# A two-layer graph network on one core: layer 1 with att applied to x1 before W, and the first layer's attention with queries on partitions

## The chip, the cores and the metric

The kernel runs on one core of a Trainium2 chip. A core has a matrix engine (TensorE, PE in the profile; its weight loads are listed apart as PEld), VectorE (DVE), ScalarE (ACT), GpSimd (POOL), a queue engine for transfers (SyncE, SP) and 16 DMA engines. [...]

The metric is the device time of one execution in microseconds, the median of several runs.

## The reference

64 batch elements of 256 tokens with 512 features, everything in float32, one 256x256 adjacency matrix for all of them. Layer 0 is masked attention with 8 heads of 64, layer 1 a graph attention with one score per token. Cut to what matters:

```python
# layer 0
q, k, v = x @ Wq + bq, x @ Wk + bk, x @ Wv + bv      # in 8 heads of 64
scores = q k^T / 8 + (1 - adj) * -1e9
out = softmax(scores) v
x1 = layernorm(x + out @ Wo + bo)

# layer 1
h = x1 @ W
s1, s2 = h @ a[:512], h @ a[512:]
e = leaky_relu(s1[:, None] + s2[None, :], 0.2) * adj
att = softmax(e)
y = layernorm(x1 + elu(att @ h + beta * h))
```

Since h = x1 W, `att @ h + beta * h` equals `((att + beta I) @ x1) @ W`, and `h @ a` equals `x1 @ (W a)`.

## The kernel before

The kernel is written with a framework that takes tiles from named pools (`bufs` is the number of buffers of a tag), finds the dependences itself and sets the semaphores. The program is unrolled completely. The order in which the steps are written gives instructions their priority; the order in which they stand on an engine in the profile is not always the written one.

One batch element goes through three parts, each a list of steps:

- `front(b)` (L141): two `tr` steps transpose the two 128-token tiles of x into xT (L126, L127) and add bo to x on GpSimd (L153); eight `qk` steps make one 128-feature block of qT or kT each (L158, evacuated by VectorE with the bias, L159); two `val` steps make v with tokens on partitions (L164, evacuated by ScalarE, L165).
- `attention(b)` (L175): for each of four head pairs a `scores` step computes k q^T, so that keys lie on partitions (L184), takes exp on ScalarE (L187) without subtracting a maximum, multiplies by the transposed 0/1 mask on GpSimd (L188) and adds the two key tiles (L190). A `mix` step multiplies by v (L200), gets the sums over keys from a product with ones (L203), and scales by their reciprocal (L204, L205); the result is written over qT. Probabilities are never transposed here. `check` (L207) keeps the largest and the least reciprocal; after the last element one branch (L373) repeats everything with `attention_general` (L218), which subtracts the row maximum, if a sum was out of range. In the profiled run the branch is not taken.
- `back(b)` (L273): two `proj` steps (product with Wo, L279; add, L280; layer norm, L131 to L138), two `flip` steps that transpose x1 into x1T, two `hidden` steps for h (L291) with the two scores of each token (L297), `edges` (L300 to L319), `flip_att` (L325), and two `last` steps: att h (L332), beta h added (L334), elu (L337 to L340), layer norm, store.

A layer norm takes the statistics and the final scaling on VectorE and, between them, the inverse root on GpSimd (L136, L137).

The loop (L352) has B + 2 = 66 passes. Pass i holds front(i), attention(i-1) and back(i-2); `merged` (L28) interleaves their steps by relative place in their own list. 62 passes hold all three parts. q, k and v biases: bq and bk are added as said; bv is folded into bo once at the start, through Wo (L115, L116).

The PSUM banks: ps_mm 3 (all products with weights), ps_sc 2 (one buffer of two banks), ps_tr 2 (transposes), ps_pv 1 (mix). The weights are loaded once through ScalarE's queue, x and the output move through SP's.

Of the kernel before, what the change touches and what calls it, by code (L numbers as in the profile page):

```python
# [8 lines left out]
F32 = mybir.dt.float32  # L9
# [5 lines left out]
P = 128  # L15
# [4 lines left out]
LARGE = 1e25  # L20
# [14 lines left out]
def gnn_two_layers(ctx: ExitStack, tc: tile.TileContext, x, adj, Wq, bq, Wk, bk, Wv, bv, Wo, bo, W, a, beta, out):  # L35
# [11 lines left out]
    ps_sc = ctx.enter_context(tc.tile_pool(name="ps_sc", bufs=1, space=PSUM))  # L47
# [11 lines left out]
    def load(b, at=None):  # L59
        X[b] = []  # L60
        for t in range(NT):
            xt = xp.tile([P, D], F32, tag="x", name=f"x_{b}_{t}")
            nc.sync.dma_start(xt, (x[b] if at is None else at)[t * P:(t + 1) * P, :])
            X[b].append(xt)
# [24 lines left out]
    bv_sb = by_partition(bv, "bv_sb")  # L89
# [7 lines left out]
    beta_sb = on_all(beta, 0, 1, "beta_sb")  # L97

# [5 lines left out]
    maskT = const.tile([P, NT, N], F32, name="maskT")  # L104
    tr = ps_tr.tile([P, NT, N], F32, tag="tr", name="tr_m")
    for k in range(NT):
        for t in range(NT):
            nc.tensor.transpose(tr[:, k, t * P:(t + 1) * P], mask_sb[:, t, k * P:(k + 1) * P], ident)
    nc.scalar.activation(maskT, tr, AF.Exp)
    ones = const.tile([P, HD], F32, name="ones")  # L110
    nc.gpsimd.memset(ones, 1.0)

    ps = ps_mm.tile([P, D], F32, tag="mm", name="ps_bo")
    for c in range(C):
        nc.tensor.matmul(ps, bv_sb[:, c:c + 1].to_broadcast([P, P]), wo_sb[:, c, :], start=c == 0, stop=c == C - 1)  # L115
    nc.vector.tensor_add(bo_sb, bo_sb, ps)  # L116

    seen = const.tile([P, 2, B], F32, name="seen")
# [22 lines left out]
    def front(b):  # L141
# [13 lines left out]
        def qk(w, bias, dst, m):  # L155
# [3 lines left out]
            nc.vector.tensor_scalar(dst[b][:, m, :], ps, bias[:, m:m + 1], None, ALU.add)  # L159

        def val(t):
# [3 lines left out]
            nc.scalar.copy(V[b][:, t, :], ps)  # L165

        steps = [lambda t=t: tr(t) for t in range(NT)]
        for m in range(C):
            steps.append(lambda m=m: qk(wq_sb, bq_sb, QT, m))
            steps.append(lambda m=m: qk(wk_sb, bk_sb, KT, m))  # L170
# [4 lines left out]
    def attention(b):  # L175
        E, S, rcp = {}, {}, {}

        def scores(hp):

            ps = ps_sc.tile([P, 2, NT, N], F32, tag="sc", name="ps_sc")  # L180
            for k in range(NT):
                for s in range(2):
                    r = s * HD
                    nc.tensor.matmul(ps[:, s, k, :], KT[b][r:r + HD, hp, k * P:(k + 1) * P],  # L184
                                     QT[b][r:r + HD, hp, :], start=True, stop=True)
            E[hp] = work.tile([P, 2, NT, N], F32, tag="E", name=f"E_{b}_{hp}", bufs=3)
            nc.scalar.activation(E[hp], ps, AF.Exp, scale=1.0 / HD ** 0.5)  # L187
            nc.gpsimd.tensor_tensor(E[hp], E[hp], maskT.unsqueeze(1).to_broadcast([P, 2, NT, N]), ALU.mult)  # L188
            S[hp] = work.tile([P, 2, N], F32, tag="S", name=f"S_{b}_{hp}", bufs=3)
            nc.gpsimd.tensor_tensor(S[hp], E[hp][:, :, 0, :], E[hp][:, :, 1, :], ALU.add)  # L190

        def mix(hp):

            if hp == 0:
                rcp[0] = work.tile([P, H // 2, N], F32, tag="rcp", name=f"rcp_{b}")
            ps = ps_pv.tile([P, 2, N], F32, tag="pv", name="ps_pv")
            for k in range(NT):
                for s in range(2):
                    h = 2 * hp + s
                    nc.tensor.matmul(ps[s * HD:(s + 1) * HD, 0, :], V[b][:, k, h * HD:(h + 1) * HD],  # L200
                                     E[hp][:, s, k, :], start=k == 0, stop=k == NT - 1)
# [207 lines left out]
```

## Time and profile before

| what | value |
|---|---|
| median of 3 runs (lowest, highest) | 3621.76 us (3616.07, 3630.26) |
| profiled run, its own time | 3621.76 us |
| its span, first to last instruction | 3620.0 us |
| mean granted TensorE clock | 0.993 |
| ScalarE busy | 886.6 us (24%) |
| HBM traffic | 39.85 MB read, 33.55 MB written, 20 GB/s |

The chain of work that ended last is spread over the engines: TensorE 39%, GpSimd 24%, gaps at issue 22%, VectorE 13%. It follows releases backward from the last instruction and changes engines many times in each of the 66 passes, so for a loop like this one it is better to take one pass apart. The costliest groups on TensorE are the q and k products (503.6 and 497.3 us, 2048 records each, two for every fp32 matmul), and the products with W, Wo and Wv (468.4, 460.6 and 460.3 us, 1024 records each). Record durations overlap: a record of the 256-column form lasts 389 ns but follows its neighbour by about 216 ns.

Views of the profile used below: the page of totals, busy times in chosen stretches, instructions in order of time, who waited for whom, and groups of instructions by line.

### The profile page before, as it was taken

The page shows a single profiled execution, that of the slowest core. Times are in us where ns is not written, and L with a number is a line of the kernel's source. Part 1 is how long each engine was busy: PE and PEld are TensorE (multiplying, and loading weights), DVE is VectorE, ACT ScalarE, POOL GpSimd, SP SyncE. Part 2 cuts the span into 40 slices and gives each one's busy share as a digit, 9 for nine tenths or more (in the row PEclk, how much of TensorE's full clock was granted, in tenths as well). Part 3 has the DMA queues.
Part 4 walks back from the last instruction along what each step waited for, and adds up shares of the span by engine and source line. Part 5 has one row for each costly group of instructions (what it writes and reads, how often), then busy time and mean ns, then how long its engine had stood idle before and what let it go on. Part 6 is the DMA issues. An engine that isn't in the chain of part 4 may idle for free.

```text
span 3620.0 us, 36170 instructions
## 1 busy us (share of the span) xinstructions
PE 3413.8 (94%) x14222; PEld 1961.9 (54%) x14222; DVE 2081.6 (58%) x3335; ACT 886.6 (24%) x1474; POOL 1409.4 (39%) x1231
## 2 busy tenths in 40 slices
PE   7999999999999999999999999999999999999996
PEld 4555555555555555555555555555555555555552
DVE  2565555565655555656555555555565555565655
ACT  1222222222222222222222222222222222222222
POOL 2443433434334334343343343433443433434332
PEclk9999999999999999999999999999999999999998
DMA  2000000000000000000000000000000000000000
GB/s 99 12 24 12 24 24 12 24 21 15 24 12 24 24 12 24 21 15 24 15 21 24 12 24 24 12 24 18 18 24 12 24 24 12 24 20 16 18 9 16
DMA packets 40319, 75.80 MB, mean 21 GB/s; under 512 B 4368, under 2 KB 4624, under 8 KB 40144
## 3 DMA queue, kind: packets, MB, share of 16 engines
q1 hardware_dynamic: 37136, 67.39, 5.5%
q10 hardware_dynamic: 2640, 5.24, 0.4%
q8 instruction: 115, 1.88, 0.2%
q0 software_dynamic: 368, 0.79, 0.1%
q14 instruction: 60, 0.49, 0.0%
HBM read 39.85 MB, written 33.55 MB: 20 GB/s over the span
## 4 chain that ended last, share of the span: by engine, by line
PE 39%; POOL 24%; issue 22%; DVE 13%; ACT 2%; POOLq 0%; ACTq 0%
POOL E L188 12%; PE ps_v L164 12%; PE ps_g L332 7%; PE ps_o L279 6%; POOL S L190 5%; DVE x L138 5%; PE ps_qk L158 3%; PE ps_sc L184 3%; DVE rcp L204 3%; PE tr_x L126 3%; POOL x L153 2%; POOL e L309 2%; POOL rs L137 2%; PE ps_pv L200 2%; ACT E L187 2%
## 5 line engine op out<-in xcount | busy, mean ns | idle before, releaser
L188 POOL TENSOR_TENSOR E<-E,maskT 128x1024 f32<-128x1024 f32 x256 | 600.7, 2347 | 834.9 <-ACT E L187 834.9
L138 DVE TENSOR_SCALAR x<-x,mv,rs 128x512 f32<-128x512 f32 x256 | 325.9, 1273 | 447.0 <-POOL rs L137 447.0
L204 DVE RECIPROCAL rcp<-ps_pv 128x256 f32<-128x256 f32 x256 | 448.2, 1751 | 152.7 <-PE ps_pv L203 152.7
L158 PE MATMUL ps_qk<-xT,wk_sb 128*128 128x256 f32 x2048 | 503.6, 389 | 0.0
L158 PE MATMUL ps_qk<-xT,wq_sb 128*128 128x256 f32 x2048 | 497.3, 386 | 0.2 <-ACT xT L127 0.2
L297 DVE SCALAR_TENSOR_TENSOR junk<-h,a_sb 128x512 f32<-128x512 f32 x256 | 192.6, 788 | 508.6 <-ACT h L293 508.6
L291 PE MATMUL ps_h<-w_sb,x1T 128*128 128x512 f32 x1024 | 468.4, 600 | 0.7 <-ACT x1T L127 0.7
L279 PE MATMUL ps_o<-wo_sb,qT 128*128 128x512 f32 x1024 | 460.6, 593 | 0.0
L164 PE MATMUL ps_v<-wv_sb,xT 128*128 128x512 f32 x1024 | 460.3, 592 | 0.0
L158 PEld LDWEIGHTS ps_qk<-xT,wk_sb 128*128 128x128 f32 x2048 | 373.4, 190 | 139.2 <-issue 99.0
L136 POOL TENSOR_SCALAR rs<-mv 128x1 f32<-128x1 f32 x256 | 56.2, 220 | 929.0 <-DVE mv L134 929.0
L187 ACT ACTIVATE E<-ps_sc 128x1024 f32<-128x1024 f32 x256 | 262.0, 1023 | 631.8 <-PE ps_sc L184 631.8
L158 PEld LDWEIGHTS ps_qk<-xT,wq_sb 128*128 128x128 f32 x2048 | 369.0, 190 | 85.5 <-DVE kT L159 23.8
L190 POOL TENSOR_TENSOR S<-E 128x512 f32<-128x512 f32 x256 | 349.5, 1365 | 15.2
L153 POOL TENSOR_TENSOR x<-x,bo_sb 128x512 f32<-128x512 f32 x128 | 184.1, 1440 | 392.2 <-PE tr_x L126 366.1
L184 PE MATMUL ps_sc<-qT,kT 64*128 64x256 f32 x2048 | 333.1, 405 | 0.1
L164 PEld LDWEIGHTS ps_v<-wv_sb,xT 128*128 128x128 f32 x1024 | 194.5, 190 | 244.0 <-issue 229.0
L291 PEld LDWEIGHTS ps_h<-w_sb,x1T 128*128 128x128 f32 x1024 | 189.5, 190 | 209.3 <-issue 204.9
L184 PEld LDWEIGHTS ps_sc<-qT,kT 64*128 64x128 f32 x2048 | 193.6, 186 | 198.2 <-issue 186.0
L200 PE MATMUL ps_pv<-E,v 128*64 128x256 f32 x2048 | 283.2, 397 | 4.5 <-DVE qT L205 3.2
L279 PEld LDWEIGHTS ps_o<-wo_sb,qT 128*128 128x128 f32 x1024 | 184.9, 190 | 185.9 <-issue 185.4
L332 PE MATMUL ps_g<-h,attT 128*128 128x512 f32 x512 | 254.7, 621 | 1.3 <-ACT attT L327 1.3
(68 smaller groups left out, 2987.2 us busy)
## 6 DMA issues: line engine op xcount, KB each, us to landing
x<-in_x_dram SPq DMA_DIRECT2D x128, 256.0 KB, 2.6
out_dram<-x SPq DMA_DIRECT2D x128, 256.0 KB, 2.0
wq_sb<-in_L_gnn_Wq_dram ACTq DMA_DIRECT2D x1, 1024.0 KB, 6.6
wk_sb<-in_L_gnn_Wk_dram ACTq DMA_DIRECT2D x1, 1024.0 KB, 14.1
wv_sb<-in_L_gnn_Wv_dram ACTq DMA_DIRECT2D x1, 1024.0 KB, 12.1
wo_sb<-in_L_gnn_Wo_dram ACTq DMA_DIRECT2D x1, 1024.0 KB, 8.8
w_sb<-in_L_gnn_W_dram ACTq DMA_DIRECT2D x1, 1024.0 KB, 9.8
a_sb<-in_L_gnn_a_dram POOLq DMA_DIRECT2D x2, 256.0 KB, 8.0
```

The source lines that it names most:

```text
L138: nc.vector.tensor_scalar(xt, xt, mv[:, 0:1], rs, ALU.subtract, ALU.mult)
L158: nc.tensor.matmul(ps, w[:, c, m * P:(m + 1) * P], XT[b][:, c, :], start=c == 0, stop=c == C - 1)
L164: nc.tensor.matmul(ps, XT[b][:, c, t * P:(t + 1) * P], wv_sb[:, c, :], start=c == 0, stop=c == C - 1)
L184: nc.tensor.matmul(ps[:, s, k, :], KT[b][r:r + HD, hp, k * P:(k + 1) * P], QT[b][r:r + HD, hp, :], start=True, stop=True)
L187: nc.scalar.activation(E[hp], ps, AF.Exp, scale=1.0 / HD ** 0.5)
L188: nc.gpsimd.tensor_tensor(E[hp], E[hp], maskT.unsqueeze(1).to_broadcast([P, 2, NT, N]), ALU.mult)
L190: nc.gpsimd.tensor_tensor(S[hp], E[hp][:, :, 0, :], E[hp][:, :, 1, :], ALU.add)
L200: nc.tensor.matmul(ps[s * HD:(s + 1) * HD, 0, :], V[b][:, k, h * HD:(h + 1) * HD], E[hp][:, s, k, :], start=k == 0, stop=k == NT - 1)
L204: nc.vector.reciprocal(rcp[0][:, hp, :], ps[:, 1, :])
L279: nc.tensor.matmul(ps, QT[b][:, c, t * P:(t + 1) * P], wo_sb[:, c, :], start=c == 0, stop=c == C - 1)
L291: nc.tensor.matmul(ps, x1T[0][:, c, t * P:(t + 1) * P], w_sb[:, c, :], start=c == 0, stop=c == C - 1)
L332: nc.tensor.matmul(ps, att[1][:, j, t * P:(t + 1) * P], hs[j], start=j == 0, stop=j == NT - 1)
```

## The change

Two things are replaced at once.

In the first layer's attention the scores have queries on partitions (the arithmetic of the old `attention_general`, with some details moved). The mask is added in PSUM's evacuation on VectorE, a row maximum is taken there, exp on ScalarE yields the row sums, GpSimd multiplies by the reciprocals, and every head's 256x256 probabilities are transposed on TensorE (four transposes each) and copied to SBUF, in turn by VectorE and ScalarE. The 1/8 scaling moves into the evacuation of q, bv into that of v (now on VectorE). Mask transpose, ones product, range check and the repeat branch are gone.

In layer 1, x1 is no longer transposed and h no longer formed. Once, at the start, W a is computed for both halves of a and spread over all partitions; the scores of a token are dot products of x1 with it, right after the layer norm. beta times the identity is added to att's diagonal blocks on GpSimd before att is transposed. `gather` multiplies x1 by att transposed, coming out with features on partitions (yT), and `last` multiplies that by W; elu reads PSUM.

```diff
-    ps_sc = ctx.enter_context(tc.tile_pool(name="ps_sc", bufs=1, space=PSUM))
+    ps_sc = ctx.enter_context(tc.tile_pool(name="ps_sc", bufs=2, space=PSUM))
...
+    beta_id = const.tile([P, P], F32, name="beta_id")
+    nc.vector.tensor_scalar(beta_id, ident, beta_sb, None, ALU.mult)
...
+    wa_sb = const.tile([P, 2, C, P], F32, name="wa_sb")
+    for i, v in enumerate((a1_sb, a2_sb)):
+        row = ps_mm.tile([P, C, P], F32, tag="mm", name="ps_wa")
+        for c in range(C):
+            junk = work.tile([P, D], F32, tag="junk", name="junk")
+            col = small.tile([P, 1], F32, tag="wa", name="wa")
+            nc.vector.scalar_tensor_tensor(junk, w_sb[:, c, :], 1.0, v, op0=ALU.mult, op1=ALU.mult, accum_out=col)
+            nc.tensor.transpose(row[:, c, :], col.to_broadcast([P, P]), ident)
+        nc.scalar.copy(wa_sb[:, i], row)
...
-            nc.scalar.copy(V[b][:, t, :], ps)
+            nc.vector.tensor_add(V[b][:, t, :], ps, bv_sb)
...
     def attention(b):
-        E, S, rcp = {}, {}, {}
...
         def scores(t, g):
             if g == 0:
-                probs[t] = pool.tile([P, H, N], F32, tag="p", name=f"p_{b}_{t}", bufs=2)
+                probs[t] = work.tile([P, H, N], F32, tag="p", name=f"p_{b}_{t}", bufs=4)
             pr = probs[t][:, 4 * g:4 * g + 4, :]

-            ps = ps_sc.tile([P, 2, 2, N], F32, tag="sc", name="ps_sg")
+            ps = [ps_sc.tile([P, 2, N], F32, tag="sc", name="ps_sc") for _ in range(2)]
             for i in range(4):
                 h, r = 4 * g + i, (i % 2) * HD
-                nc.tensor.matmul(ps[:, i % 2, i // 2, :], QT[b][r:r + HD, h // 2, t * P:(t + 1) * P],
+                nc.tensor.matmul(ps[i % 2][:, i // 2, :], QT[b][r:r + HD, h // 2, t * P:(t + 1) * P],
                                  KT[b][r:r + HD, h // 2, :], start=True, stop=True)
             for s in range(2):
-                nc.vector.scalar_tensor_tensor(pr[:, s::2, :], ps[:, s], 1.0 / HD ** 0.5,
-                                               mask_sb[:, t:t + 1, :].to_broadcast([P, 2, N]),
-                                               op0=ALU.mult, op1=ALU.add)
+                nc.vector.tensor_add(pr[:, s::2, :], ps[s], mask_sb[:, t:t + 1, :].to_broadcast([P, 2, N]))
             nm = small.tile([P, 4], F32, tag="nm", name="nm")
             nc.vector.tensor_reduce(nm, pr, AX.X, ALU.max, negate=True)
...
-            pT[h] = pool.tile([P, NT, N], F32, tag="pT", name="pT", bufs=4)
+            pT[h] = work.tile([P, NT, N], F32, tag="pT", name="pT", bufs=6)
...
-    def back(b, to):
-        hs, x1T, s, att = {}, {}, {}, {}
+    def back(b):
+        s, att, yT = {}, {}, {}
...
             nc.vector.tensor_add(X[b][t], X[b][t], ps)
             layernorm(X[b][t])
-
-        def flip(t):
...
-        def hidden(t):
...
             s[t] = small.tile([P, 2], F32, tag="s", name="s")
-            for i, v in enumerate((a1_sb, a2_sb)):
+            for i in range(2):
                 junk = work.tile([P, D], F32, tag="junk", name="junk")
-                nc.vector.scalar_tensor_tensor(junk, hs[t], 1.0, v, op0=ALU.mult, op1=ALU.mult,
-                                               accum_out=s[t][:, i:i + 1])
+                nc.vector.scalar_tensor_tensor(junk, X[b][t], 1.0, wa_sb[:, i].rearrange("p c k -> p (c k)"),
+                                               op0=ALU.mult, op1=ALU.mult, accum_out=s[t][:, i:i + 1])
...
+                d = e[:, t, t * P:(t + 1) * P]
+                nc.gpsimd.tensor_tensor(d, d, beta_id, ALU.add)
...
+        def gather(g):
+
+            if g == 0:
+                yT[0] = work.tile([P, C, N], F32, tag="yT", name=f"yT_{b}")
+            ps = ps_mm.tile([P, 2, N], F32, tag="mm", name="ps_y")
+            for i in range(2):
+                m = 2 * g + i
+                for j in range(NT):
+                    nc.tensor.matmul(ps[:, i, :], X[b][j][:, m * P:(m + 1) * P], att[1][:, j, :],
+                                     start=j == 0, stop=j == NT - 1)
+            nc.scalar.copy(yT[0][:, 2 * g:2 * g + 2, :], ps)
+
         def last(t):
-            ps = ps_mm.tile([P, D], F32, tag="mm", name="ps_g")
-            for j in range(NT):
-                nc.tensor.matmul(ps, att[1][:, j, t * P:(t + 1) * P], hs[j], start=j == 0, stop=j == NT - 1)
-            u = work.tile([P, D], F32, tag="u", name="u")
-            nc.vector.scalar_tensor_tensor(u, hs[t], beta_sb, ps, op0=ALU.mult, op1=ALU.add)
+            ps = ps_mm.tile([P, D], F32, tag="mm", name="ps_u")
+            for c in range(C):
+                nc.tensor.matmul(ps, yT[0][:, c, t * P:(t + 1) * P], w_sb[:, c, :], start=c == 0, stop=c == C - 1)
...
-            nc.scalar.activation(m, u, AF.Relu, scale=-1.0)
+            nc.scalar.activation(m, ps, AF.Relu, scale=-1.0)
...
-            nc.vector.scalar_tensor_tensor(u, u, 0.0, m, op0=ALU.max, op1=ALU.add)
-            nc.vector.scalar_tensor_tensor(X[b][t], u, -1.0, X[b][t], op0=ALU.add, op1=ALU.add)
+            nc.vector.scalar_tensor_tensor(m, ps, 0.0, m, op0=ALU.max, op1=ALU.add)
+            nc.vector.scalar_tensor_tensor(X[b][t], m, -1.0, X[b][t], op0=ALU.add, op1=ALU.add)
...
+        steps = [lambda t=t: proj(t) for t in range(NT)] + [edges, flip_att]
+        return steps + [lambda g=g: gather(g) for g in range(C // 2)] + [lambda t=t: last(t) for t in range(NT)]
```

The exp, the reciprocal and the normalisation of `scores`, and the functions `flip` and `mix`, are those of `attention_general` in the kernel before (L235 to L262). The list of the attention's steps, too: four `scores`, then `flip` of heads 0 to 7 with the `mix` of a pair one pair behind. A pass now has 16 attention steps, 12 of the front and 8 of the back.

## The prediction

> **What bounds the kernel now.** I read the engine totals and the 40 slices first, then the busy times of one steady round, then that round on TensorE in order of time, then the waits and the groups.
>
> ```profile
> PE 3413.8 (94%) x14222; PEld 1961.9 (54%) x14222; DVE 2081.6 (58%) x3335; ACT 886.6 (24%) x1474; POOL 1409.4 (39%) x1231
> PE   7999999999999999999999999999999999999996
> DMA  2000000000000000000000000000000000000000
> ```
>
> TensorE is full in every slice but the first and the last; the DMA engines are idle after the first. The kernel repeats one round per batch element, so one round is priced:
>
> ```profile
> 2023.40:2078.70 55.30, 52.91 (x223) 30.48 (x222) 32.50 (x53) 13.81 (x23) 21.98 (x19) 1.00 0.06 19
> 2078.70:2134.00 55.30, 52.90 (x223) 30.48 (x222) 32.49 (x53) 13.81 (x23) 21.98 (x19) 1.00 0.06 20
> ```
>
> Columns: stretch, length, busy PE, PEld, DVE, ACT, POOL. A round takes 55.3 us, two in a row alike. Of the 66 passes of the loop, 62 hold all three parts: 62 x 55.3 = 3429 of 3620.0 us; 191 us are start and end.
>
> ```profile
> 2072.91 1.13 PE L184 MATMUL ps_sc<-qT,kT 64*128 64x256 f32 x6
> 2075.40 0.72 PE L325 MATMUL tr_a<-ident,e 128*128 128x128 f32 x4 [1.36 <-DVE e L318]
> ...
> 2099.41 0.60 PE L126 MATMUL tr_x<-ident,x 128*128 128x128 f32 x4
> 2099.94 1.08 PE L200 MATMUL ps_pv<-E,v 128*64 128x256 f32 x8
> 2100.85 0.60 PE L203 MATMUL ps_pv<-S,ones 128*64 128x256 f32 x4
> 2101.38 1.99 PE L158 MATMUL ps_qk<-xT,wk_sb 128*128 128x256 f32 x8
> 2104.40 0.63 PE L126 MATMUL tr_x<-ident,x 128*128 128x128 f32 x4 [1.02 <-DVE x L138]
> ```
>
> Matmuls overlap, so I price one by the distance from start to start ("slot"): 8 records of ps_pv 0.91 us, 4 of ones 0.53, 8 of ps_qk 1.83, 4 transposes 0.43 to 0.53. TensorE stands still twice a round, 1.36 and 1.02 us, 2.4 together; the other 52.9 us are work. Also seen: six of the eight score records of the *next* round stand ahead of tr_a. The issued order is thus not the written one: later work that is ready is put into a hole.
>
> ```profile
> DVE x L138 <- POOL rs L137: 447.0, 256, 4.1
> PE tr_a L325 <- DVE e L318: 93.9, 64, 5.6
> PE tr_x L126 <- DVE x L138: 69.1, 64, 3.0
> ```
>
> VectorE loses 447 us / 256 = 1.75 us at each layer norm to GpSimd, yet little of it reaches TensorE, since VectorE has 22.8 us of slack in a round.
>
> ```profile
> L188 POOL TENSOR_TENSOR E<-E,maskT 128x1024 f32<-128x1024 f32 x256 | 600.7, 2347 | 834.9 <-ACT E L187 834.9
> L138 DVE TENSOR_SCALAR x<-x,mv,rs 128x512 f32<-128x512 f32 x256 | 325.9, 1273 | 447.0 <-POOL rs L137 447.0
> L204 DVE RECIPROCAL rcp<-ps_pv 128x256 f32<-128x256 f32 x256 | 448.2, 1751 | 152.7 <-PE ps_pv L203 152.7
> L280 DVE TENSOR_TENSOR x<-x,ps_o 128x512 f32<-128x512 f32 x128 | 87.1, 681 | 27.2 <-PE ps_o L279 27.2
> L210 DVE TENSOR_REDUCE seen<-rcp 128x1 f32<-128x1024 f32 x64 | 77.3, 1208 | 0.0
> L314 ACT ACTIVATE e<-e,nm 128x256 f32<-128x256 f32 x128 | 63.9, 500 | 389.5 <-DVE nm L311 389.5
> ```
>
> These six rows are the prices of what goes and comes: busy total, mean ns of one, idle time before.
>
> [...] from 2093.60 to 2097.67 VectorE waits for rs, and the add of ps_o, whose matmuls ended by 2096.5, runs only at 2099.08. [...] the 8 half-width records of ps_pv take 0.91 us, four full-width slots. No run here shows what happens when the two heads do not alternate. [...] here the granted clock is 0.59 in the last 20 us, where TensorE waits most.
>
> **The change part by part, per round.** The words name layer 1, but the diff also gives up the first layer's attention with keys on partitions: scores come out with queries on partitions, get mask and row maximum on VectorE, a normalisation on GpSimd, and each head is transposed on TensorE.
>
> TensorE. The two x1 flips (8 transposes) go: -1.0. 32 transposes of probabilities come: 32 x 0.109 (the distance of two) = 3.5, plus about 0.06 at each of 8 group changes (0.53 against 0.43): +4.0. The ones matmuls go, but the mix now does head s=0 entirely before s=1: its slot lies between 1.0 us (pairing kept: 4 x 0.216 + 0.14 of switching) and 1.87 (8 x 0.216 + 0.14), against 0.91 + 0.53 = 1.44 now. I take 1.24, pairing partly kept, since pairing survives two passes of one head now: 4 x -0.2 = -0.8, bounds -1.8 and +1.7. ps_g (4 matmuls of 512) becomes gather (8 of 256): two slots of 1.83 for 1.82 and 1.71: +0.1. The product with W keeps its 8 matmuls of 512. Sum +2.3 (bounds +0.8 and +5.1): work 55.2 us. So TensorE's work alone already fills the present round.
>
> VectorE. Gone: 4 reciprocals 7.0, 4 multiplies 1.65, the check's reduction 1.2, two u 1.5: -11.4. New: 8 mask adds at 0.68 = 5.4; 4 row maxima over 128x1024 at 1.21 = 4.8; 4 small reciprocals 0.4; 4 copies of 128x512 from PSUM, not shown, between 0.47 (the 256 form, L159) and 0.68 (L280), taken 0.65 = 2.6; 4 copies of 128x256 at 0.41 = 1.65; two value-bias adds 1.4. +16.3, so 32.5 becomes 37.4. The two score dot products stay, from x1 instead of h.
>
> ScalarE: -8.8 (4 exponentials of 1.02, six copies, the check), +11.7 (16 exponentials at a step of 0.51, 4 head copies, 2 yT copies): 13.8 to 16.7. GpSimd: -14.8 (mask multiply and pair sum), +9.4 (4 normalisations of 128x1024 at 2.35), +0.75 (two beta adds on 128x128, scaled from L309's 1.27 for 512): 22.0 to 17.3. Both stay far from the round. SP's queue and the two loads and two stores of a round don't change.
>
> What counts is where VectorE's work lies. From the first scores to the transposes of att it must do 4 x 2.7 (two adds, maximum, reciprocal), two projections at 4.2 (add, statistics, 1.27 normalisation, two dot products), edges 3.1, about four biases 1.6 and two head copies 1.3: 25.2 us. TensorE's own steps there are 4 scores 4.3, transposes 1.0, projections 7.0, four q/k 7.3, three head flips 1.5, tr_s 0.2: 21.3. VectorE is 3.9 us longer in this stretch before any wait; two layer-norm waits add 3.5, so TensorE could stand up to 7.4. Each score step needs the two banks that VectorE's adds free; behind a waiting reciprocal (four exponentials, about 2.1 us) or normalisation stand those adds, the biases that free the three ps_mm banks, and the head copies that free ps_tr. Later q, k and v steps (14 to 18 us that need only xT) can be pulled in, as the scores are now. That cover holds while a bank is free; I let it hide about two thirds, leaving 2.7 us. The x1 flip's 1.0 goes, tr_a's 1.4 stays: waits 2.4 become 4.1. Round: 55.2 + 4.1 = 59.3, +4.0.
>
> Start and end. Before, the first q product starts at 32.86, because ps_bo waits in TensorE's queue for wo until 25.07. ScalarE cannot copy xT before about 20 (its table load is at 18.02), so up to 12 us can be won; but W times a, which waits for w_sb (issued at 17.6, 9.8 to land) and eight 0.79 us products, may stand ahead: gain 0 to 12, taken 6. At the end the longer score chain and the shorter layer-1 chain about cancel (+1). Sum -5.
>
> Total: 3620.0 + 62 x 4.0 - 5 = 3863 of span, plus the 1.8 us that lie outside it in the profiled run (3621.76, which is also the median of the three): 3865.
>
> **Rivals.** (a) TensorE's work alone: the cover holds all, waits stay 2.4. Round 57.6: 3620 + 62 x 2.3 - 5 + 2 = 3760. For it: little of 447 us of VectorE waiting reaches TensorE today. Against: scores now leave PSUM through VectorE. (b) VectorE's queue sets the round: every wait in the head counts. In the written order the head is 41 us (four score blocks of 5.0 with their exponentials, two projections of 6 with GpSimd's normalisation before rs, edges 8) and 36 us of TensorE work follow: 77. Halfway between that and the 55.2 of pure work is 66: 3620 + 62 x 10.7 - 5 + 2 = 4280[...]. For it: the FIFO evidence. Against: reordering. (c) Faster: the list order fills every hole. The pairs survive (work +0.8, 53.7) and, with the x1 flip gone and more steps between edges and tr_a, waits fall to 0.5: round 54.2, 3620 - 62 x 1.1 - 5 + 2 = 3549. It decides once waits fall below 2.4 - 0.8 = 1.6 us. For it: the slack of VectorE over the whole round is still 18 us. Against: the head's 25.2 against 21.3.
>
> **How the numbers follow.** A change within 0.5% (18 us) cannot be told from none here. Forecast 0.42, (a) 0.25, (b) 0.24, (c) 0.09. The forecast's own range is 3770 to 3960. Range 3650 to 4250: below, (a) with the low TensorE bound (+0.8: 3667); above, nearly (b). Faster 0.07, same 0.03 (the edge of (c)), slower 0.90.
>
> **What would show it.** In the changed profile: 32 head transposes a round in slots near 0.5; the mix's slot, which settles the pairing; VectorE near 37 us a round; TensorE's work 55 us and its waits on VectorE's score adds, normalised x and head copies, 4 us in all, lying in the first half of the round. Waits under 2 us or a VectorE that never holds a bank would make me wrong on one side; TensorE under 85% busy on the other.

## The result: 9.5% slower

| | before | after |
|---|---|---|
| median of 4 runs (lowest, highest) | 3624.41 us (3616.07, 3630.26) | 3966.69 us (3966.34, 3967.94) |
| span of the profiled run | 3620.0 us | 3964.6 us |
| mean granted TensorE clock | 0.993 | 0.973 |
| one round, mean of the steady ones | 55.5 us | 61.0 us |
| TensorE's waits in such a round | 2.4 us | 4.3 us |

The ratio is 1.095, 95% interval 1.092 to 1.097. The forecast was 3865 us, slower, range 3650 to 4250: the direction is right, the time lies inside, 102 us above the forecast.

The engine totals of the changed kernel and TensorE's row of the 40 slices:

```profile
PE 3637.0 (92%) x15240; PEld 2244.0 (57%) x15240; DVE 2231.8 (56%) x4307; ACT 1072.0 (27%) x3139; POOL 980.0 (25%) x1102
PE   7999999999999999999999999999999999999996
```

TensorE still sets the time in every slice but the first and the last. Its busy share is two points lower and its instructions are 1018 more. Two successive rounds of the changed kernel, from one first score product to the same product a round later (stretch, length, then busy PE, PEld, DVE, ACT, POOL, then the granted clock):

```profile
1984.56:2045.84 61.28, 56.99 (x241) 35.21 (x239) 34.74 (x67) 16.71 (x49) 15.22 (x18) 0.97 0.06 18
2045.84:2106.05 60.21, 55.49 (x241) 33.81 (x239) 34.57 (x67) 16.70 (x49) 15.23 (x18) 1.00 0.05 18
```

The second one ran at full clock from end to end, so it is the one to set against the 55.30 us of before: 2.6 us more work and about 2.3 us more waiting. The first has a clock of 0.97 and waits of 4.3 us, 0.4 less: the one of 0.44 us at tr_a is not there, and the granted clock stands at 0.5 from 2008.1 to 2011.5 us ahead of it. Taken between successive tr_a, 60.1 us is met once in eight rounds; the other seven take 60.9 to 61.3. TensorE in the full-clock round, in order of time:

```profile
2053.09 1.79 PE L181 MATMUL ps_sc<-kT,qT 64*128 64x256 f32 x8 [0.45 <-DVE p L184]
...
2062.01 0.55 PE L198 MATMUL tr_p<-ident,p 128*128 128x128 f32 x3 [0.45 <-POOL p L192]
2062.39 1.89 PE L153 MATMUL ps_qk<-xT,wk_sb 128*128 128x256 f32 x8
2064.12 0.27 PE L241 MATMUL tr_s<-ident,s 128*128 128x128 f32 x1
2067.77 0.32 PE L241 MATMUL tr_s<-ident,s 128*128 128x128 f32 x1 [3.37 <-DVE junk L235]
2067.93 1.03 PE L153 MATMUL ps_qk<-xT,wq_sb 128*128 128x256 f32 x4
...
2072.62 1.09 PE L210 MATMUL ps_pv<-pT,v 128*64 128x256 f32 x8
2073.64 1.99 PE L153 MATMUL ps_qk<-xT,wq_sb 128*128 128x256 f32 x8
2075.56 0.65 PE L210 MATMUL ps_pv<-pT,v 128*64 128x256 f32 x2
2076.64 0.74 PE L266 MATMUL tr_a<-ident,e 128*128 128x128 f32 x4 [0.44 <-POOL e L259]
```

Four waits, 4.7 us in all, and one of them is nearly everything: 3.37 us in front of the second of the two tr_s, the transposes that spread the token scores over all partitions. The tr_a and tr_x waits of before are gone but for 0.44. The second tr_s stands directly behind the first, with nothing between. It waits for `junk`, the product whose accumulator is the second tile's token score. VectorE in that stretch, and below it GpSimd:

```profile
2063.95 0.55 DVE L133 TENSOR_SCALAR x<-x,mv,rs 128x512 f32<-128x512 f32 x1 [0.99 <-POOL rs L132]
2064.41 0.17 DVE L191 RECIPROCAL rc<-sm 128x4 f32<-128x4 f32 x1
2064.49 0.66 DVE L184 TENSOR_TENSOR p<-ps_sc,mask_sb 128x512 f32<-128x512 f32 x1
2065.07 2.02 DVE L235 SCALAR_TENSOR_TENSOR junk<-x,wa_sb 128x512 f32<-128x512 f32 x1
...
2067.03 0.68 DVE L235 SCALAR_TENSOR_TENSOR junk<-x,wa_sb 128x512 f32<-128x512 f32 x1
```

```profile
2064.65 1.89 POOL L192 TENSOR_TENSOR p<-p,rc 128x1024 f32<-128x1024 f32 x1 [0.74 <-DVE rc L191]
```

Two products of the same shape take 2.02 and 0.68 us. The slow one starts 0.42 us after GpSimd's normalisation of four heads has started and ends 0.55 us after that has ended at 2066.54. Over the whole run, 63 of the 256 products start while a normalisation is running and take 2.02 to 2.03 us (one that starts 0.94 us into it 1.50); the other 193 take 0.68 to 0.69. The groups of the changed kernel give the means (busy total, mean ns, idle before):

```profile
L192 POOL TENSOR_TENSOR p<-p,rc 128x1024 f32<-128x1024 f32 x256 | 484.6, 1893 | 547.2 <-DVE rc L191 547.2
L235 DVE SCALAR_TENSOR_TENSOR junk<-x,wa_sb 128x512 f32<-128x512 f32 x256 | 249.7, 1011 | 0.1
L133 DVE TENSOR_SCALAR x<-x,mv,rs 128x512 f32<-128x512 f32 x256 | 139.8, 546 | 251.6 <-POOL rs L132 251.6
```

1011 ns is one product of 2.02 and three of 0.68, so one of the four products of a round meets the normalisation (starts while it runs), and it stands in the chain that TensorE waits for. The 546 ns of the layer norm's scaling (L133) show the same from the other side. In the kernel before its mean of 1273 ns was a mixture: in a round two scalings took 0.55 us, one 1.48 beside GpSimd's pair addition (L190) and one 2.56 beside the mask multiply (L188). From the round of before:

```profile
2097.60 1.27 POOL L190 TENSOR_TENSOR S<-E 128x512 f32<-128x512 f32 x1
2097.67 1.49 DVE L138 TENSOR_SCALAR x<-x,mv,rs 128x512 f32<-128x512 f32 x1 [4.07 <-POOL rs L137]
...
2101.62 2.34 POOL L188 TENSOR_TENSOR E<-E,maskT 128x1024 f32<-128x1024 f32 x1
2101.69 2.56 DVE L138 TENSOR_SCALAR x<-x,mv,rs 128x512 f32<-128x512 f32 x1 [0.99 <-POOL rs L137]
```

### The profile page after: what moved, and what is told of

Same layout as the page of the kernel before. It is cut to its first block, busy times and chain, and to the rows that moved or that the text cites. A ratio compares the mean times of both kernels' runs of the same rounds, so it can differ in the third digit from the quotient of the medians.

```text
span 3964.6 us, 40122 instructions
## 1 busy us (share of the span) xinstructions
PE 3637.0 (92%) x15240; PEld 2244.0 (57%) x15240; DVE 2231.8 (56%) x4307; ACT 1072.0 (27%) x3139; POOL 980.0 (25%) x1102
## 4 chain that ended last, share of the span: by engine, by line
PE 69%; DVE 19%; POOL 7%; issue 3%; DMA 1%; ACT 0%; SPq 0%; POOLq 0%; DVEq 0%
PE ps_qk L153 17%; PE ps_u L285 11%; PE ps_v L159 11%; PE ps_pv L210 8%; DVE junk L235 6%; PE ps_y L278 6%; PE tr_p L198 6%; PE ps_o L229 5%; DVE p L184 3%; DVE nm L186 2%; DVE x L230 2%; POOL p L192 2%; POOL x L148 2%; POOL rs L132 2%; DVE x L133 2%
## 5 line engine op out<-in xcount | busy, mean ns | idle before, releaser
L189 ACT ACTIVATE p<-p,nm 128x256 f32<-128x256 f32 x1024 | 507.6, 497 | 490.0 <-DVE nm L186 490.0
L192 POOL TENSOR_TENSOR p<-p,rc 128x1024 f32<-128x1024 f32 x256 | 484.6, 1893 | 547.2 <-DVE rc L191 547.2
L285 PE MATMUL ps_u<-w_sb,yT 128*128 128x512 f32 x1024 | 466.7, 599 | 0.0
L198 PE MATMUL tr_p<-ident,p 128*128 128x128 f32 x2048 | 364.5, 300 | 30.1 <-POOL p L192 29.6
L198 PEld LDWEIGHTS tr_p<-ident,p 128*128 128x128 f32 x2048 | 267.9, 153 | 172.3 <-issue 65.3
L210 PE MATMUL ps_pv<-pT,v 128*64 128x256 f32 x2048 | 361.5, 394 | 0.9 <-DVE qT L212 0.9
L181 PE MATMUL ps_sc<-kT,qT 64*128 64x256 f32 x2048 | 333.7, 402 | 29.3 <-DVE p L184 29.1
L184 DVE TENSOR_TENSOR p<-ps_sc,mask_sb 128x512 f32<-128x512 f32 x512 | 335.3, 676 | 1.2 <-PE ps_sc L181 1.0
L203 DVE COPY pT<-tr_p 128x512 f32<-128x512 f32 x256 | 173.9, 679 | 267.8 <-PE tr_p L198 267.6
L186 DVE TENSOR_REDUCE nm<-p 128x4 f32<-128x1024 f32 x256 | 310.7, 1214 | 2.2
L285 PEld LDWEIGHTS ps_u<-w_sb,yT 128*128 128x128 f32 x1024 | 189.3, 190 | 211.7 <-issue 184.5
## 6 DMA issues: line engine op xcount, KB each, us to landing
wk_sb<-in_L_gnn_Wk_dram ACTq DMA_DIRECT2D x1, 1024.0 KB, 14.5
```

The source lines that it names most:

```text
L181: nc.tensor.matmul(ps[i % 2][:, i // 2, :], QT[b][r:r + HD, h // 2, t * P:(t + 1) * P], KT[b][r:r + HD, h // 2, :], start=True, stop=True)
L184: nc.vector.tensor_add(pr[:, s::2, :], ps[s], mask_sb[:, t:t + 1, :].to_broadcast([P, 2, N]))
L186: nc.vector.tensor_reduce(nm, pr, AX.X, ALU.max, negate=True)
L189: nc.scalar.activation(pr[:, i, :], pr[:, i, :], AF.Exp, bias=nm[:, i:i + 1], accum_out=sm[:, i:i + 1])
L192: nc.gpsimd.tensor_tensor(pr, pr, rc.unsqueeze(2).to_broadcast([P, 4, N]), ALU.mult)
L198: nc.tensor.transpose(tr[:, k, t * P:(t + 1) * P], probs[t][:, h, k * P:(k + 1) * P], ident)
```

## The experiments

All times below are set against runs of the kernel before made alongside (medians 3619.46 for the first four experiments in the table, 3623.73 for the next four, 3623.81 for the last four). Round, TensorE's waits and half clock are means over the steady rounds between 1000 and 3000 us, in us per round; half clock is the time for which the granted clock stood at 0.5.

| run | median us | ratio (95%) | round | waits | half clock |
|---|---|---|---|---|---|
| before | 3624.41 | 1 | 55.5 | 2.4 | 0.4 |
| after | 3966.69 | 1.095 (1.092 to 1.097) | 61.0 | 4.3 | 3.0 |
| e1_edges_later | 4060.09 | 1.122 (1.120 to 1.124) | 62.4 | 5.1 | 3.5 |
| e2_keys_att_new_l1 | 3853.13 | 1.065 (1.063 to 1.067) | 59.2 | 5.1 | 4.6 |
| e2b, the same with edges later | 3776.13 | 1.043 (1.041 to 1.045) | 58.0 | 2.6 | 6.8 |
| e3_new_att_old_l1 | 3981.20 | 1.100 (1.098 to 1.102) | 61.4 | 3.0 | 6.8 |
| e4_fill_wait | 4076.64 | 1.126 (1.124 to 1.128) | 62.8 | 4.7 | 1.3 |
| e5_norm_on_vector | 3802.14 | 1.049 (1.048 to 1.051) | 58.3 | 1.1 | 0.0 |
| e6_no_row_max | 3816.72 | 1.054 (1.052 to 1.055) | 58.6 | 3.8 | 1.9 |
| e8_head_copies_on_scalar | 3964.10 | 1.093 (1.090 to 1.096) | 61.0 | 4.8 | 5.1 |
| e9_before_edges_later | 3563.46 | 0.984 (0.982 to 0.985) | 54.5 | 2.0 | 0.0 |
| e10_before_mask_on_vector | 3479.86 | 0.960 (0.959 to 0.962) | 53.3 | 0.6 | 0.0 |
| e11_norm_on_scalar | 3808.57 | 1.051 (1.050 to 1.053) | 58.5 | 2.5 | 0.5 |
| e12, e2 with the mask on VectorE | 3566.15 | 0.984 (0.983 to 0.986) | 54.6 | 2.3 | 2.2 |

The theories, in the order in which they came: the load on VectorE in the first half of the round holds TensorE up (the prediction's own); TensorE's added work is the loss; the place of `edges` among the steps, too near behind the layer norm, makes the 3.4 us pause; the granted clock, which falls after that pause, makes part of it; and, after the first results, GpSimd's long multiply, which VectorE and the layer norm wait for. The experiments follow by question.

**Which half of the change costs what?** e2 keeps the attention of before and takes layer 1 of after; e3 is the reverse. In e2, e2b and e12 the range check's final branch, which the profiled run of before doesn't take, is left out.

```diff
e2: kernel before, with wa_sb, beta_id and back(b) of the changed kernel
e3: changed kernel, with back(b, to) of the kernel before
```

> The attention of the kernel before (keys on partitions, no head transposed) with the changed layer 1 alone; the final branch on the range check is left out. Theory A (the attention part of the change costs TensorE 3.5 us of work a round, the layer-1 part saves about 0.9 us of it and costs only the wait for the token scores): TensorE work about 52.0 us a round, waits 2 to 4 us, time 3560 to 3680 us. Rival C (the reordered layer 1 is itself the loss): round over 57 us, time over 3740 us.

> The attention of the changed kernel with the layer 1 of the kernel before (x1 transposed, h formed, scores from h). Theory A: TensorE work about 56.4 us a round (52.9 plus 3.5), the 3.4 us wait before tr_s gone because the scores come a step earlier relative to edges, waits 2.5 to 4 us, time 3830 to 3950 us. Rival C: without the reordered layer 1 the time is near that of the kernel before, under 3720 us.

The attention alone (e3) costs 3981.2 - 3619.5 = 362 us, layer 1 alone (e2) 234 us; together they cost 342. They don't add up, so neither is a price by itself: each moves waits of the other, and the clock as well, as the half-clock column shows. In e2 TensorE's work really falls, from 52.9 to 52.1 us in the full-clock round from 1956.45 to 2013.93, as one x1 flip less per tile should make it. It is slower all the same. TensorE of e2, in order of time:

```profile
2060.80 0.27 PE L249 MATMUL tr_s<-ident,s 128*128 128x128 f32 x1
2063.40 0.32 PE L249 MATMUL tr_s<-ident,s 128*128 128x128 f32 x1 [2.33 <-DVE junk L243]
...
2072.93 1.12 PE L274 MATMUL tr_a<-ident,e 128*128 128x128 f32 x4 [3.05 <-POOL e L267]
```

Without flips of x1 and products for h between the layer norm and the token scores, two waits meet TensorE in a round, 5.1 us instead of 2.4, and 4.6 us a round are at half clock: the four transposes of tr_a, behind the second wait, last 1.12 us here and 0.72 before. In e3 the loss lies elsewhere. TensorE, then VectorE, then GpSimd of e3:

```profile
2054.52 1.99 PE L140 MATMUL ps_qk<-xT,wq_sb 128*128 128x256 f32 x8
2059.38 2.73 PE L168 MATMUL ps_sc<-kT,qT 64*128 64x256 f32 x8 [2.87 <-DVE p L171]
```

```profile
2054.76 0.55 DVE L120 TENSOR_SCALAR x<-x,mv,rs 128x512 f32<-128x512 f32 x1 [2.71 <-POOL rs L119]
...
2058.57 0.18 DVE L178 RECIPROCAL rc<-sm 128x4 f32<-128x4 f32 x1 [0.82 <-ACT p L176]
2058.67 0.66 DVE L171 TENSOR_TENSOR p<-ps_sc,mask_sb 128x512 f32<-128x512 f32 x1
```

```profile
2050.89 1.89 POOL L179 TENSOR_TENSOR p<-p,rc 128x1024 f32<-128x1024 f32 x1 [4.54 <-DVE rc L178]
...
2052.93 1.26 POOL L135 TENSOR_TENSOR x<-x,bo_sb 128x512 f32<-128x512 f32 x1
```

Here is the mechanism that the prediction described, a score add (L171) that frees a score bank and stands behind a waiting layer norm and a waiting reciprocal. In the changed kernel itself it costs 0.45 us a round. GpSimd has a part in it here too: the 2.71 us are a wait for rs, and rs stands in GpSimd's queue behind the normalisation and the addition of bo. But the wait of 2.87 us is only 0.5 more than the two waits of before together, and the round is 5.9 us longer. The rest is the added work of TensorE and the clock: by the granted share of 0.5, an estimate, 6.8 us at half clock cost at most 3.4 us a round.

**Is it where `edges` stands?**

```diff
-        steps = [lambda t=t: proj(t) for t in range(NT)] + [edges, flip_att]
+        steps = [lambda t=t: proj(t) for t in range(NT)] + [lambda: None, edges, flip_att]
```

> The changed kernel with one empty step between proj and edges in the list of the back, so that the transposes of the token scores (tr_s) stand later in TensorE's order, behind one more q product and one head flip (about 2.3 us). Theory A (the second tr_s waits 3.4 us in place for VectorE's token scores, and the pause also cools TensorE's clock in most rounds): the wait falls to about 1 us, the half-clock stretches go, the round falls from 61.0 to about 57.7 us, time about 3760 us. Rival B (VectorE's load in the first half of the round is the bound, so the wait only moves to another place): round at least 60 us, time above 3900 us.

> The old attention with the changed layer 1, and edges one place later. Theory A: TensorE work 52.0 us a round and waits of about 1.5 us: round 53.5 us, time about 3510 us, less than both kernels. Rival B: nothing gained over the version without the empty step.

> The kernel before with an empty step ahead of edges and one ahead of flip_att in the list of the back, so that tr_s and tr_a stand later on TensorE. If the 1.4 us wait before tr_a is only a matter of the place: round 54.0 us, about 3540 us. If the chain moves with it: 3624 us or more.

An empty step delays `edges` by one place. (e9 has one ahead of `edges` and one ahead of `flip_att`.) In the kernel before it wins 60 us and in e2 77, but in the changed kernel it loses 93, as rival B of its expectation had it. The pause in front of tr_s stays and only changes its reason. TensorE and then VectorE of e1:

```profile
2047.84 1.89 PE L153 MATMUL ps_qk<-xT,wq_sb 128*128 128x256 f32 x8
2052.25 0.43 PE L241 MATMUL tr_s<-ident,s 128*128 128x128 f32 x2 [2.52 <-DVE pT L203]
```

```profile
2048.35 2.02 DVE L235 SCALAR_TENSOR_TENSOR junk<-x,wa_sb 128x512 f32<-128x512 f32 x1
...
2051.52 0.67 DVE L203 COPY pT<-tr_p 128x512 f32<-128x512 f32 x1
```

tr_s now waits for a transpose bank, whose owner, a transposed head, waits for VectorE's copy (L203); and that copy stands in VectorE's queue behind the same 2.02 us product. So the pause is not cured by time between the steps.

**Is it the load on VectorE?** e8 moves all head copies to ScalarE and takes 2.5 us a round off VectorE. e6 leaves out the row maximum, four VectorE instructions of 1.2 us a round, and subtracts zero in its place.

```diff
e8:
-            if h % 2:
-                nc.scalar.copy(pT[h], tr)
-            else:
-                nc.vector.tensor_copy(pT[h], tr)
+            nc.scalar.copy(pT[h], tr)
e6:
-            nc.vector.tensor_reduce(nm, pr, AX.X, ALU.max, negate=True)
+            nc.gpsimd.memset(nm, 0.0)
```

> The changed kernel with all eight head copies out of PSUM on ScalarE, none on VectorE: VectorE has 4 x 0.68 us less a round, and the two transpose banks no longer wait behind VectorE's queue. Theory A: round about 59.3 us, time about 3860 us. Rival E: above 3930 us.

> The changed kernel without the row maximum of the first layer's scores (zero is used in its place, so that part is left out): VectorE has 4 x 1.21 us less a round and each score step's chain is 1.2 us shorter; TensorE's work is the same. Theory A: waits fall from 4.7 to 2.5 us or less a round, the clock stays up, round 58 us, time about 3780 us. Rival E (clash with GpSimd, not the amount of VectorE work): above 3900 us.

e8 gains nothing: 3964 against 3967, and tr_s waits 3.4 us as before. It is not a clean test of the time: the mixes take 4.1 us of TensorE a round instead of 5.3, since none is torn apart any more (see the work of TensorE further down), and its few rounds at full clock take 59.4 us instead of 60.1. The clock takes this back, with 5.1 us a round at half instead of 3.0. What e8 does show is that the wait in front of tr_s does not depend on the head copies.

e6 gains 150 us, near to what theory A had forecast for it. Its two tr_s follow each other as in the changed kernel:

```profile
2045.10 0.32 PE L241 MATMUL tr_s<-ident,s 128*128 128x128 f32 x1 [0.67 <-DVE junk L235]
```

The wait is 2.7 us shorter. The product for the token scores takes 686 ns on average instead of 1011, so the meeting with GpSimd is gone, and that is 1.3 of the 2.7. The other 1.4 come from VectorE's queue: without the row maxima it starts the second tile's scaling 1.0 us ahead of the first tr_s instead of 0.2, and no score add stands between the scaling and the products. So what VectorE has to do ahead of the second token score does count. But new waits of 1.7 us at tr_a and 1.0 at tr_p take the gain back, and the waits are still 3.8 us; the larger part of the 2.4 us that the round gains is whole mixes (1.2 us) and less time at half clock.

**Is it GpSimd's normalisation?** e5 gives it to VectorE, e11 to ScalarE (four instructions, one per head, with rc as scale).

```diff
e5:
-            nc.gpsimd.tensor_tensor(pr, pr, rc.unsqueeze(2).to_broadcast([P, 4, N]), ALU.mult)
+            nc.vector.tensor_tensor(pr, pr, rc.unsqueeze(2).to_broadcast([P, 4, N]), ALU.mult)
e11:
-            nc.gpsimd.tensor_tensor(pr, pr, rc.unsqueeze(2).to_broadcast([P, 4, N]), ALU.mult)
+            for i in range(4):
+                nc.scalar.activation(pr[:, i, :], pr[:, i, :], AF.Copy, scale=rc[:, i:i + 1])
```

> The changed kernel with the normalisation of the probabilities on VectorE instead of GpSimd: VectorE gets about 4 x 1.2 us more a round, and no long GpSimd instruction runs beside its two-input products (one of them took 2.02 us instead of 0.68 us in the round that was read). Theory A (the amount of VectorE work in the first half of the round sets the waits): waits grow, time above 3990 us. Rival E (the clash with GpSimd makes the token scores late): the wait before tr_s falls by 1.3 us or more and the clock recovers, time below 3900 us.

> The changed kernel with the normalisation of the probabilities on ScalarE, four instructions of 128x256 at a step of about 0.5 us: as long as GpSimd's one of 1.89 us, so the chain of a score step is not shorter; VectorE's work stays as in the changed kernel, and GpSimd has no long instruction left in the first half of the round. Theory E (the loss beyond the added TensorE work comes from GpSimd: it stretches VectorE's two-input products and holds rs behind it): time 3740 to 3830 us, like the version with it on VectorE, clock 0.99. Rival A (VectorE's load and the length of the chain): 3920 us or more.

e5 adds 2.7 us a round to VectorE (37.4 against 34.7) and gains 165 us. That is the opposite of what VectorE's total load as the cause would give. Its groups, and TensorE around the token scores:

```profile
L192 DVE TENSOR_TENSOR p<-p,rc 128x1024 f32<-128x1024 f32 x256 | 311.7, 1218 | 2.1
L235 DVE SCALAR_TENSOR_TENSOR junk<-x,wa_sb 128x512 f32<-128x512 f32 x256 | 165.4, 683 | 0.1
```

```profile
2039.03 0.27 PE L241 MATMUL tr_s<-ident,s 128*128 128x128 f32 x1
2039.14 1.89 PE L153 MATMUL ps_qk<-xT,wq_sb 128*128 128x256 f32 x8
2040.87 1.89 PE L153 MATMUL ps_qk<-xT,wk_sb 128*128 128x256 f32 x8
2043.54 0.32 PE L241 MATMUL tr_s<-ident,s 128*128 128x128 f32 x1 [0.78 <-DVE junk L235]
```

Two things have changed at once: no product of 2.02 us any more, and a q and a k product that now stand between the two tr_s and cover the way from one to the other. e11 parts them, since there the two tr_s follow each other as in the changed kernel:

```profile
2040.85 0.27 PE L242 MATMUL tr_s<-ident,s 128*128 128x128 f32 x1
2043.21 0.32 PE L242 MATMUL tr_s<-ident,s 128*128 128x128 f32 x1 [2.09 <-DVE junk L236]
```

```profile
L236 DVE SCALAR_TENSOR_TENSOR junk<-x,wa_sb 128x512 f32<-128x512 f32 x256 | 164.3, 679 | 0.1
```

The same order on TensorE, the same instructions in VectorE's queue, the product at 0.68 instead of 2.02, and the wait is 2.09 instead of 3.37: 1.28 us shorter, where the product became 1.34 us shorter. So of the 3.4 us pause, 1.3 are the meeting with GpSimd, shown; the other 2.1 are what stands in VectorE's queue up to the second token score (the scaling, a reciprocal, a score add, two products) while nothing stands between the two tr_s. The framework chose that order. That it did so because it takes VectorE and GpSimd for faster than they are would fit, but no run here shows it.

**Is it the clock?** e4 puts six products whose result nobody uses between the two tr_s.

```diff
+                if t == 0:
+                    for _ in range(6):
+                        nc.tensor.matmul(row[:, N:2 * N], s[0][:, 1:2].to_broadcast([P, P]), w_sb[:, 0, 0:N],
+                                         start=True, stop=True)
```

> The changed kernel with six idle-time matmuls of 128x256 (2.6 us, into an unused part of the same PSUM bank) between the first and the second transpose of the token scores, where TensorE stands still for 3.4 us a round; their result is not used. Theory D (the pause is what halves TensorE's granted clock for 3.4 us afterwards in seven rounds of eight, worth about 0.85 us a round): the clock stays near 1.00, the round falls from 61.0 to about 60.2 us, time about 3915 us although TensorE has 2.6 us more to do. Rival (the half-clock stretches have nothing to do with the pause, or the pause does not matter): time 3967 us or more.

TensorE of e4:

```profile
1993.20 2.75 PE L244 MATMUL tr_s<-w_sb,s 128*128 128x256 f32 x12
1996.74 0.32 PE L241 MATMUL tr_s<-ident,s 128*128 128x128 f32 x1 [0.78 <-DVE junk L235]
...
2005.34 0.74 PE L270 MATMUL tr_a<-ident,e 128*128 128x128 f32 x4 [2.08 <-POOL e L263]
```

The pause is filled as meant, 3.4 to 0.8 us, and the half clock falls from 3.0 to 1.3 us a round; but the order of the other instructions changed with it, new waits of 2.1 us at tr_a and 0.9 more at tr_p appear, and the kernel is 110 us slower. As a test of the clock it is inconclusive. The changed kernel's own rounds are the better evidence. After its pause in the round before the one shown above:

```profile
2006.50 0.32 PE L241 MATMUL tr_s<-ident,s 128*128 128x128 f32 x1 [3.38 <-DVE junk L235]
...
2008.29 1.92 PE L153 MATMUL ps_qk<-xT,wq_sb 128*128 128x256 f32 x4
```

Four records of ps_qk take 1.92 us here and 1.03 at 2067.93, after the same pause. The granted clock stands at 0.5 for 3.4 us in this round, from 2008.1 to 2011.5, and so it does in seven rounds of eight; the eighth, which has the pause and not the drop, is 0.8 to 1.2 us shorter. Between 1000 and 3000 us all 29 half-clock stretches of the changed kernel and all five of the kernel before last 3.413 us. In the changed kernel one begins 61.44 us after the one before, 18 times 3.413, or 119.47 us, 35 times, where a round is spared.

Divide the changed kernel between 1000 and 3000 us into stretches of 3.413 us, counted from its drops. In each of the 29 stretches ahead of a drop TensorE stands idle for 1.84 us or more; in the other 527 at full clock it does so for 1.74 at most. The pause moves against this grid, as seven rounds of about 61 us and one of 60.1 are not whole multiples of 3.413, and the spared round is the one whose pause the grid cuts into 1.7 and 1.7 us. These are estimates, as the ends of TensorE's records are modelled, and no exact border: the kernel before dropped its clock five times after stretches with 1.4 to 1.6 us of idle time. In the other runs slower records stand behind pauses of 2.6 to 3.1 us: in e2 the four of tr_a take 1.12 us instead of 0.72 after 3.05 us, in e3 the eight of ps_sc 2.73 instead of 1.79 after 2.87, in e2b the four of tr_a 1.11 after 2.64.

In e2b successive tr_s lie 58.03 us apart, 17 times 3.413, and in e3 61.44, 18 times; in both 6.8 us of a round are at half clock. That their length is therefore no plain sum of work and waits is the author's reading and not shown.

**Does the finding hold in the kernel before?** Its own long GpSimd multiply (L188, the mask) is moved to VectorE, in it and in e2.

```diff
-            nc.gpsimd.tensor_tensor(E[hp], E[hp], maskT.unsqueeze(1).to_broadcast([P, 2, NT, N]), ALU.mult)
+            nc.vector.tensor_tensor(E[hp], E[hp], maskT.unsqueeze(1).to_broadcast([P, 2, NT, N]), ALU.mult)
```

> The kernel before with the multiplication of E by the mask on VectorE instead of GpSimd. Theory E: the two waits of 2.4 us a round, both behind a layer norm or the att chain, shrink to about 1 us: round 54 us, time about 3540 us, less than the kernel before. Rival A (more VectorE work makes it later): 3630 us or more.

> The old attention with the changed layer 1, and the multiplication of E by the mask on VectorE instead of GpSimd (4 x 1.2 us more for VectorE, 4 x 2.35 us less for GpSimd). Theory E: the waits of 2.3 us before tr_s and 3.0 us before tr_a shrink to about 2 us together, the clock recovers, round about 54.5 us, time about 3570 us. Rival A: 3853 us or more.

e10 takes 3479.9 us: 4.0% faster than the kernel before, and the fastest of all kernels here. Its groups and one round:

```profile
L188 DVE TENSOR_TENSOR E<-E,maskT 128x1024 f32<-128x1024 f32 x256 | 357.2, 1395 | 149.0 <-ACT E L187 149.0
L138 DVE TENSOR_SCALAR x<-x,mv,rs 128x512 f32<-128x512 f32 x256 | 140.7, 550 | 323.2 <-POOL rs L137 323.2
```

```profile
2046.65:2099.95 53.30, 52.70 (x223) 30.57 (x223) 34.51 (x57) 13.81 (x23) 12.44 (x15) 1.00 0.06 20
```

VectorE does 2 us a round more than before and TensorE waits 0.6 us instead of 2.4. The layer norm's scaling, 1273 ns on average in the kernel before, is 550 here, VectorE waits 323 us for rs in all instead of 447, and the wait of tr_x is gone. The multiply's mean of 1395 ns is above the 1227 ns that the same multiply takes on VectorE in e12; what makes it longer here is not shown. e12 takes 3566 us, 287 less than e2. So with the long multiply off GpSimd, layer 1 reordered without the new attention goes from 6.5% slower to 1.6% faster than the kernel before; but against e10, which has the same attention and the old layer 1, it is 86 us slower. In none of the pairs is the reordered layer 1 by itself a clear gain: with the new attention it saves 14.5 us, 0.4% (e3 to after).

## Why the prediction came out as it did

**The work of TensorE: right, in its sum and in most terms.** Predicted +2.3 us a round, measured 52.9 to 55.5, +2.6. From the distances of starts in the two full-clock rounds, waits taken off:

```
term                         before  after   change  predicted
transposes of heads (tr_p)    0      3.98    +3.98     +4.0
x and x1 flips (tr_x)         1.91   1.14    -0.77     -1.0
mix (ps_pv)                   5.76   5.29    -0.47     -0.8
ps_h+ps_g / ps_y+ps_u        10.60  10.53    -0.07     +0.1
all others                   34.66  34.56    -0.10      0
```

The mix was the uncertain one, a slot taken as 1.24 us between 1.0 and 1.87. Four mixes now take 5.29 us, 1.32 on average, but no single one looks like that. Three are at 1.02 (2072.62 above: eight half-width records in the time of four), so pairing survives although each head is written as a whole before the other. One is torn into groups of two, two and four records (from 2075.56 on, others between), 0.64, 0.58 and 1.01: 2.2 us, more than the 1.83 of eight full-width records, so with no pairing at all. Whether the framework or TensorE puts the two halves in turn in the other three is not shown. In e6 and e8 all four mixes are whole and take 4.1 us together; what tears one apart in the changed kernel was not tested.

**VectorE's load: right as to place, wrong as to size, and its total not the limit.** Predicted 37.4 us a round, measured 34.7. The four layer-norm scalings were carried over at 1.27 us and take 0.55 now, 4 x 0.73 = 2.9 us less. That this is about the whole difference is chance: the product beside GpSimd takes 1.3 us more than its price, and the records of VectorE overlap by about 1 us more. The mean of 1.27 belonged to what ran on GpSimd beside two of the four, not to the operation. GpSimd's normalisation, too, was priced at 2.35 us from L188 and takes 1.89.

**The waits: nearly right in sum, wrong in their parts.** Predicted 4.1 us a round, of which tr_a's 1.4 stay and 2.7 come from score adds, normalised x and head copies. Measured 4.3 on average: tr_s 3.4, score products 0.45, tr_p 0.45, tr_a 0.06. That the two sums are near each other is luck, as four fifths of the measured one stand at a place that the forecast does not name. "The x1 flip's 1.0 goes" was right, "tr_a's 1.4 stays" was wrong, and the step that "TensorE could stand up to 7.4" because VectorE's 25.2 us exceed TensorE's 21.3 in the head of the round is the one that fails. With 2.7 us more on VectorE (e5) the waits fall to 1.1 us, with the same VectorE instructions but nothing of the normalisation on GpSimd (e11) to 2.5, and with 2.5 us less on VectorE (e8) they are 4.8. What stands in its place is one chain, second layer norm, products with W a, second tr_s: what lies in VectorE's queue within and ahead of this chain counts (e6), the total does not. The prediction kept its two dot products ("The two score dot products stay") at their old price and did not ask what now lies between the layer norm and tr_s: flips and h before, nothing after. And it put GpSimd aside as "far from the round" because its busy total is small, where the total was not what counted.

**The clock: missing from the forecast.** It entered none of its sums. TensorE's busy time grows from 53.1 to 56.7 us on average, 3.6, of which 2.6 are work as counted in full-clock rounds; so about 1.0 us a round, an estimate, is the slower clock and records stretched by it.

**Start and end:** predicted -5 us. The first q product starts at 32.55 instead of 32.86, since eight transposes for W a, held by VectorE's products with w_sb, stand among those of x; nothing was won. Outside 62 mean rounds lie 3964.6 - 62 x 61.0 = 182.6 us, against 3620.0 - 62 x 55.5 = 179.

**The sum.** 62 x 5.5 + 4 = 345 us of span, as measured (344.6), against 62 x 4.0 - 5 = 243 predicted. The 5.5 are 2.6 of work, 1.9 of waits and 1.0 of clock, where the forecast had 2.3, 1.7 and none.

**The rivals.** (a), all waits covered, would have been 3760; e5, with waits of 1.1 us, comes to 3802, since its work rises to 57.3 us (its mixes take 6.1 us and its scores 6.1 instead of 4.9). (b), VectorE's queue setting the round, did not happen: 61.0 against 66. (c), faster because pairs survive and waits fall, had its first half (three mixes of four) and not the second.

What stays open: how much of e5's and e10's gain comes from GpSimd's multiply no longer running beside VectorE's work and how much from the order of instructions that came with the edit, since only at tr_s in e11 are the two apart; and what the slower clock costs in each run, since no run took the drop away and left the rest as it was.

## What to carry to other kernels

When a step between a producer and its consumer is removed, look at what then stands between them on the engine that sets the time: the step may have been the cover for a chain on other engines. Before a duration is carried over from a profile, look at its minimum and maximum (545 and 2566 ns where the forecast took 1273) and at what ran on GpSimd beside it. Here a VectorE product took 2.02 us instead of 0.68 beside GpSimd's 128x1024 multiply, a place that no busy total shows. Try such a multiply on VectorE even where VectorE is the busier of the two: in e5 that took 165 us off the changed kernel, in e10 144 off the kernel before.

## What the runs showed of the hardware

- In the changed kernel a 128x512 VectorE product of two SBUF tiles took 0.68 to 0.69 us when no GpSimd multiply was running at its start (193 of 256) and 2.02 us when it started 0.42 us after a 128x1024 GpSimd multiply. With that multiply moved to ScalarE (e11) its mean was 0.68. A 128x512 scaling of one SBUF tile by two columns took 0.55 us in the changed kernel, and in the kernel before 1.48 us when it started 0.07 us after a 128x512 GpSimd addition and 2.56 us when it started 0.07 us after a 128x1024 multiply.
- A 128x1024 multiply took 1.89 us on GpSimd with a column broadcast as second operand and 2.35 with a mask tile; on VectorE the first took 1.22 on average (e5), the second 1.23 in e12 and 1.40 in e10.
- All half-clock stretches of the two kernels between 1000 and 3000 us lasted 3.413 us and began, within each kernel, whole multiples of 3.413 us apart. In the changed kernel, at full clock, a drop followed every stretch of 3.413 us on this grid in which TensorE stood idle for 1.84 us or more and none with 1.74 or less; in the kernel before five followed 1.4 to 1.6 us. One round in eight was spared, and was 0.8 to 1.2 us shorter.
- Eight records of two 64-column halves took 1.02 us, eight full-width ones of ps_qk 1.83, although the four of one half are written ahead of the other's. What puts them in turn is not shown.
